# A two-layer decoder on one core: decayed scores kept in PSUM, one round a unit in layer 1 self-attention, and a copy pinned to its place

## The chip, the core and the metric

The kernel runs on one core of a Trainium2 chip. The core has a matrix engine (PE, TensorE), a vector engine (DVE, VectorE), an activation engine (ACT, ScalarE), a general engine (POOL, GpSimd) and an engine that here only issues transfers (SP, SyncE). Each works through its own instructions in order and waits on semaphores for the others. Data lie in device memory, in SBUF (128 partitions), or in PSUM, the memory into which PE writes and from which DVE and ACT read its products. The profile lists PE's weight loads as a line of their own, PEld, since they overlap the matmuls.

The metric is the time of one execution in device microseconds. The time before is the median of three runs. One further execution was recorded by the profiler; every duration here is from that one.

## What is computed

The input is 8 sequences of 512 tokens with 256 features, and for each a context of 64 rows. Two decoder layers follow, each with three sub-blocks, and after each sub-block a layernorm of the sum of its input and its output:

```python
x = layernorm(x + L0_attn(x, ...))    # 16 heads of 16, latent keys and values, decay
x = layernorm(x + L0_xattn(x, ctx, ctx, mask))
x = layernorm(x + L0_ffn(x, ...))     # butterfly products around a gelu
x = layernorm(x + L1_attn(x, ...))    # 16 heads of 64, causal, rotary, latent keys and values
x = layernorm(x + L1_xattn(x, ctx, ...))  # 8 heads of 64 over 512 + 64 keys
x = layernorm(x + L1_ffn(x, ...))     # 8 experts, the best 2 of each token
```

What matters here of the three sub-blocks that the change touches:

```python
# L0_attn: the decay multiplies the scores before the softmax
scores = einsum('bhqd,bhkd->bhqk', qh, k_rec) / sqrt(d)
decay = exp(-0.01 * abs(t[:, None] - t[None, :]))
attn = softmax(scores * decay)

# L1_attn: q and k are rotated, scores are causal
q = q * cos + rotate_half(q) * sin
scores = einsum('bhsd,bhtd->bhst', q, k) / sqrt(64) + causal
out = einsum('bhst,bhtd->bhsd', softmax(scores), v)

# L1_ffn: each token goes to two experts, weighted
w, idx = top_k(softmax(logits / 1.5), 2)
```

## The kernel before

The program is written in stages: layer 0 self-attention (about 22 to 800 us of the span), layer 0 context attention and feed-forward (to 1222), layer 1 self-attention (to 2105), layer 1 context attention with the routing of tokens to experts in it (to 2935), the experts (to 3464), and the last stores. In most stages PE's instructions run in the order in which the program writes them (`manual_schedule` for PE). On the other engines a scheduler places instructions by its own estimate of when their inputs are ready, and it can move one ahead of others; `keep_in_program_order` around an instruction holds it where it is written. Tiles come from pools: a tag has a number of buffers, and the next tile of the tag waits until the buffer's old content has had its last reader.

**Layer 0 self-attention.** A unit is a sequence b and a group g of four heads, 32 units. Each unit goes through `l0_project` (q and k, s_qk), `l0_maxima` for four query tiles i, `l0_shift`, then for four key tiles kt `l0_probs` and `l0_values`, and `l0_finish`. The units are interleaved: step kt of unit n does `l0_probs` of unit n, `l0_values` of the step before, and `l0_maxima` of unit n+2; then one piece of another unit, `l0_shift` (transposes tM, L463), `l0_finish` (transposes tO, L520), `l0_project` (s_qk, L415 and L416), or a part of an output projection (tT L539, o_out L547) or of the preparation of the next sequence (tT L378, o_lat L386).

`l0_maxima` (L423) computes scores for 128 queries against 512 keys, four heads as two pairs. Each pair has one PSUM tile s_sc of two banks. On DVE one `tensor_tensor_reduce` for each head (L437) multiplies by the decay table, writes the decayed scores to SBUF (`scored`) and the row's maximum to mx. After both pairs, one `tensor_tensor` (L447) takes the diagonal 128x128 blocks of all four heads less the maxima into diag. `l0_probs` (L472) later puts the transposed scores of two pairs into two PSUM tiles s_st: off the diagonal they are computed afresh with the decay factored into the rows (L481 and L484, with kf, kr, qf, qr, which POOL multiplies out in L468), on the diagonal diag is transposed in (L486). ACT exponentiates them to pt (L490), and `l0_values` multiplies (L501). s_sc, s_st and s_qk take turns in three two-bank PSUM buffers. POOL in this stage also multiplies out the butterfly factors for the feed-forward (L308), which it runs nearly without pause.

Ahead of the first unit, the product o_wlat of two weights is copied to `wlat` by DVE (L586), and o_lat (L386) needs it.

**Layer 1 self-attention.** A unit is a sequence b and a pair c of heads, 64 units. The four query tiles form groups m: tiles 0 and 1, tile 2, tile 3 (`GROUPS`). `l1_scores` (L939) makes s_sc (L949) and the softmax: DVE adds the mask and takes the maximum (L279), ACT exponentiates (L290), DVE scales (L926). `l1_transposes` transposes p on PE (tP, L981) and copies with ACT (L982). `l1_values` (L995) multiplies with v (o_pv, L1005), after the last group `out_done` copies to aT, and after the last pair of a sequence an output projection follows (o_out, L248) in two pieces that are put off, and with it residual and layernorm on DVE and POOL. `l1_prepare` makes q and k (s_q, L880 and L881), their rotation on DVE (L885, L886) and by four accumulating transfers from POOL's queue (L889), and v (t_v, L896). A unit is done in two steps: step 0 does group 0, step 1 groups 1 and 2. In each step PE does the scores, a piece of preparation (`l1_pre`: s_q of the unit two on, or t_v of the next one), the transposes of the step before, and the values of the step before that.

**Layer 1 context attention.** 128 steps of s_sc (L1130), a softmax, transposes (tP, copied to pt by DVE and ACT at L108 and L110) and o_pv (L1164, L1172), with projections of the next unit (t_qk L1084, k completed by POOL copies at L1092, t_v L1097). The routing of sequence b is done in pieces among the steps of sequence b+1. `route_norm` (L1216) writes the layernorm into z, which has one buffer. `route_picks` (L1271) writes the expert weights into z (L1282) and the token numbers (L1283, a copy of 4 columns from `tokens_at`, which is there from the start). `route_places` (L1286) finds rows and sends z out with eight indirect transfers from POOL's queue (rows_in, L1307). The experts' loads of rows_in (xr, L1430) follow all those they need.

Of the kernel before, what the change touches and what calls it, by code (L numbers as in the profile page):

```python
# [11 lines left out]
F32 = mybir.dt.float32  # L12
I32 = mybir.dt.int32
AF = mybir.ActivationFunctionType
ALU = mybir.AluOpType
# [3 lines left out]
P = 128  # L19
# [30 lines left out]
def decoder_kernel(ctx: ExitStack, tc: tile.TileContext, a: dict, out: bass.AP):  # L50
# [35 lines left out]
    def slot(name):  # L86
        return ring.tile([P, SLOT], F32, tag="slot", name=name)
# [335 lines left out]
    def l0_maxima(b, g, i):  # L423


        q, k = live["qk", b, g]
        mx = live["mx", b, g]
        for pair in range(2):
            s = s_tile("s_sc")
            for j in range(2):  # L430
                h = 32 * (2 * pair + j)
                pe.matmul(  # L432
                    s[:, j, :], lhsT=q[h : h + 32, i * P : (i + 1) * P], rhs=k[h : h + 32, :], start=True, stop=True
                )
            for j in range(2):
                h = 2 * pair + j
                dve.tensor_tensor_reduce(  # L437
                    out=scored[:, h, :],
                    in0=s[:, j, :],
                    in1=decay[:, i, :],  # L440
                    scale=1.0,
                    scalar=-3.0e38,
                    op0=ALU.mult,
                    op1=ALU.max,
                    accum_out=mx[:, i, h : h + 1],
                )
        dve.tensor_tensor(  # L447
            live["diag", b, g][:, i],
            scored[:, :, i * P : (i + 1) * P],
            mx[:, i, :].unsqueeze(2).to_broadcast([P, 4, P]),  # L450
            ALU.subtract,
        )

    def l0_shift(b, g):

# [100 lines left out]
    with tc.tile_pool(name="bfly", bufs=1, side="right") as bfly, phase("l0_self") as ph, psum("a", 3, 1, 1):  # L556

        vaug = [ph.tile([P, NT, 288], F32, name=f"vaug{n}", bufs=1) for n in range(2)]
        mneg = ph.tile([P, NT, P], F32, name="mneg", bufs=1)
        pool.memset(mneg, 0.0)  # L560
        for n in range(2):
            pool.memset(vaug[n], 1.0)

        scored = slot("scored").rearrange("p (h n) -> p h n", h=4)
        diags = [slot(f"diag{i}").rearrange("p (i h n) -> p i h n", i=NT, h=4) for i in range(2)]
        bias_row = bfly.tile([1, 1024], F32, name="bias_row")
        sp.dma_start(out=bias_row, in_=a["ff_bexp"].rearrange("(o n) -> o n", o=1))
        butterfly = butterfly_ops(bfly, bias_row)
        units = [(b, g) for b in range(NB) for g in range(4)]
        later, scalings = [], []  # L570
        with tc.manual_schedule(engines={PE}):
            turn0, turn1, latent, values = l0_prepare(0)
            turn0()
            turn1()
            dve.tensor_tensor(wkT, wkT, wvT, ALU.add)
            o = o_tile("o_wlat")
            for c in range(KC):
                for k in range(KC):
                    pe.matmul(
                        o[:, c * 64 : (c + 1) * 64],  # L580
                        lhsT=wkT[:, k, c * P : (c + 1) * P],
                        rhs=wdown[:, k, :],
                        start=(k == 0),
                        stop=(k == KC - 1),
                    )
            dve.tensor_copy(wlat.rearrange("p c n -> p (c n)"), o[:, 0 : KC * 64])  # L586
            latent()
            l0_project(*units[0])

            between = [values, partial(l0_project, *units[1])]  # L590
            for i in range(NT):
                l0_maxima(*units[0], i)
                if between:
                    between.pop(0)()
            l0_shift(*units[0])
            l0_project(*units[2])

            for i in range(2):
                l0_maxima(*units[1], i)
        for n, (b, g) in enumerate(units):  # L600

            maxima = [(*units[n + 2], i) for i in range(NT)] if n + 2 < len(units) else []
            if n == 0:
                maxima = [(*units[1], i) for i in range(2, NT)] + maxima
            if g == 0 and b + 1 < NB:
                later.extend(l0_prepare(b + 1))
            for kt in range(NT):
                l0_probs(b, g, kt)

                if kt:  # L610
                    l0_values(b, g, kt - 1)
                elif n:
                    l0_values(*units[n - 1], NT - 1)
                for _ in range(-(-len(maxima) // (NT - kt))):
                    l0_maxima(*maxima.pop(0))

                if kt == 1 and n + 1 < len(units):
                    l0_shift(*units[n + 1])
                if kt == 1:

                    if scalings:
                        scalings.pop(0)(tc.keep_in_program_order)
                elif kt == 2:
                    if n:
                        l0_finish(*units[n - 1])
                        if g == 0:
                            later.extend(l0_output(b - 1))
                else:
                    if kt and n + 3 < len(units):
                        l0_project(*units[n + 3])  # L630
                    if later:
                        later.pop(0)()
                for _ in range(3 - kt % 2):
                    next(butterfly, None)
        l0_values(*units[-1], NT - 1)
        l0_finish(*units[-1])
        later.extend(l0_output(NB - 1))
        for piece in later:
            piece()
        for scaling in scalings:  # L640
            scaling()
        for _ in butterfly:
            pass
        o = o_tile("o_bias")
        for f in range(8):
            pe.matmul(o[:, f : f + 1], lhsT=bias_row[0:1, f * P : (f + 1) * P], rhs=one, start=True, stop=True)
        dve.tensor_tensor(upb, o[:, 0:8], upb, ALU.add)
# [258 lines left out]

    GROUPS = ((0, 1), (2,), (3,))

    STEPS = ((0,), (1, 2))

    def l1_pre(b, c, step):

        at = units.index((b, c))
        if step == 0 and at + 2 < len(units):
            pieces_of[units[at + 2]].pop(-2)()
        if step == 1 and at + 1 < len(units):
            pieces_of[units[at + 1]].pop()()
        if c == 5 and b + 1 < NB:
            pieces_of[b + 1, 0].pop(0)()

    def scaled(p, sums, n):

        rsum = col("rsum", 4)
# [3 lines left out]

    put_off = []

    def groups(stage):  # L930


        def run(b, c, step):
            for m in STEPS[step]:
                stage(b, c, m)

        return run

    def l1_scores(b, c, m):  # L939
        q, k, _ = live["qkv", b, c]  # L940
        s = s_tile("s_sc")
        p = p_tile(bufs=4)
        sums = col("sums", 4)
        at = 0
        for i in GROUPS[m]:
# [46 lines left out]
            if then:  # L992
                then(b)

    def l1_values(b, c, m):  # L995
        pt = live.pop(("pt", b, c, m))
        _, _, v = live["qkv", b, c]
        if m == 0:
            live["o", b, c] = o_tile("o_pv")
        o = live["o", b, c]  # L1000
        n = 0
        for k, block in enumerate(l1_blocks(m)):
            cols = slice(block[0][0] * P, (block[-1][0] + 1) * P)
            for j in range(2):
                pe.matmul(  # L1005
                    o[64 * j : 64 * (j + 1), cols],
                    lhsT=v[:, k, 64 * j : 64 * (j + 1)],
                    rhs=pt[:, j, n : n + len(block), :].rearrange("p k n -> p (k n)"),
                    start=(k == 0),
                    stop=(k == GROUPS[m][-1]),  # L1010
                )
            n += len(block)
        if m == len(GROUPS) - 1:
            out_done(b, c, live.pop(("o", b, c)), woT1, 8, lambda: xs[b])

    with phase("l1_self") as ph, tc.manual_schedule(engines={PE}):
        for u, what in ((0, 0), (0, 0), (0, 0), (0, 0), (1, 0)):
            pieces_of[units[u]].pop(what)()
        _pipeline(
            [(b, c, step) for b in range(NB) for c in range(8) for step in range(len(STEPS))],  # L1020
            [
                (0, groups(l1_scores)),
                (0, l1_pre),
                (1, groups(l1_transposes)),
                (2, groups(l1_values)),
            ],
            put_off,
        )


    q1_k1 = slot("q1_k1")
# [239 lines left out]
    def route_picks(b):  # L1271
# [8 lines left out]
        both, z = picked[:, 0:NT, :], live["z", b]  # L1280
        dve.tensor_tensor(both, picks[0], picks[1], ALU.add)
        dve.tensor_tensor(z[:, :, D : D + NE], both, pr, ALU.mult)  # L1282
        dve.tensor_copy(z[:, :, D + NE], tokens_at[:, b * NT : (b + 1) * NT])  # L1283
        live["picks", b] = picks, picked

    def route_places(b):  # L1286
# [358 lines left out]
```

## Time and profile before

| | us |
|---|---|
| median of 3 runs | 3511.45 (3504.51 to 3514.59) |
| profiled execution | 3503.39 |
| its span | 3501.7 |
| layer 0 self-attention, stretch 100 to 750 | 650 |
| layer 1 self-attention, 1222 to 2105 | 883 |
| layer 1 context attention, 2105 to 2935 | 830 |
| PE busy in the span | 3299.3 (94%) |
| DVE / ACT / POOL busy | 2087.4 (60%) / 1510.5 (43%) / 1118.1 (32%) |
| mean granted PE clock | 0.973 of full speed |

In the lines that follow, a row of a list of instructions in time has its start and its duration in us, the engine, the source line, the operation, the tile written and the tiles read, shapes, how many instructions of one kind were put together (x4), and in brackets the idle time of the engine before it with what ended it. A row of the waits has the waiting engine and line, what it waited for, the sum in us, how often, and the longest. A share of busy time is an average over stages with different limits; what a stage gains or loses is read inside it.

### The profile page before, as it was taken

To read this page: it belongs to the slowest core of one execution; us is meant where nothing else is said; L and a number is where in the kernel's file an instruction comes from. 1 tells how busy PE (TensorE), PEld (TensorE's weight loads), DVE (VectorE), ACT (ScalarE), POOL (GpSimd) and SP (SyncE) were. 2 spreads that over 40 slices of the span, in tenths; PEclk is the share of its full clock that TensorE was granted. 3 is DMA by queue.
4 is the path that set the end of the run, shared out by engine and by line. 5 is a ranking of instruction groups with operands and counts; after the bars stand their busy time and mean duration, and the time that the engine had idled before them with its cause. 6 is when DMAs were issued, how large, how long until landed. Compare 5 with 4: busy or idle time off the path is not lost. (4 is left out here: it accounts for less than half of the span.)

```text
span 3501.7 us, 52528 instructions
## 1 busy us (share of the span) xinstructions
PE 3299.3 (94%) x19574; PEld 2080.0 (59%) x19574; DVE 2087.4 (60%) x5710; ACT 1510.5 (43%) x3139; POOL 1118.1 (32%) x1032
## 2 busy tenths in 40 slices
PE   7999999998999989999999999999999999999995
PEld 3344344445666656666666665555555556888884
DVE  5777777767666467677776775666666664111112
ACT  2444444453344255565555663444444343222222
POOL 3888788862211122222222210011111111222222
PEclk8999999998999999999999999999999999999997
DMA  4001011110000099232322320000000004666674
GB/s 134 25 25 33 21 35 42 40 63 13 2 2 1 13 252 243 37 43 37 42 39 37 43 43 4 10 13 22 19 19 19 10 19 167 193 188 181 188 229 138
DMA packets 166002, 234.96 MB, mean 67 GB/s; under 512 B 26570, under 2 KB 128650, under 8 KB 165747
## 3 DMA queue, kind: packets, MB, share of 16 engines
q1 hardware_dynamic: 139010, 175.83, 15.9%
q0 software_dynamic: 25584, 51.57, 10.3%
q10 hardware_dynamic: 1152, 4.19, 0.3%
q8 instruction: 156, 2.56, 0.3%
q14 instruction: 100, 0.81, 0.1%
HBM read 135.83 MB, written 61.11 MB: 56 GB/s over the span
## 5 line engine op out<-in xcount | busy, mean ns | idle before, releaser
L437 DVE CUSTOM_DVE_ANT_0 scored<-s_sc,decay 128x512 f32<-128x512 f32 x512 | 323.0, 687 | 179.6 <-PE s_sc L432 178.8
L290 ACT ACTIVATE p<-p,nm 128x128 f32<-128x128 f32 (+3 forms) x512 | 282.5, 553 | 301.9 <-DVE nm L279 300.4
L889 POOL DMA_DIRECT2D qk<-turned x256 | 208.2, 1231 | 591.8 <-issue 296.0
L490 ACT ACTIVATE pt<-s_st 128x1024 f32<-128x1024 f32 x256 | 261.9, 1024 | 278.4 <-PE s_st L486 250.3
L926 DVE TENSOR_SCALAR p<-p,rsum 128x576 f32<-128x576 f32 (+4 forms) x768 | 300.3, 433 | 10.0
L1135 ACT ACTIVATE p<-s_sc,nm 128x576 f32<-128x576 f32 x256 | 189.6, 743 | 222.3 <-DVE nm L1134 201.3
L1501 DVE TENSOR_SCALAR y<-o_y,share 128x256 f32<-128x256 f32 x71 | 34.3, 484 | 408.6 <-PE o_y L1481 408.6
L1464 PE MATMUL s_h<-xnT,we 128*128 128x256 f32 (+1 forms) x1248 | 260.3, 362 | 0.0
L279 DVE CUSTOM_DVE_ANT_0 p<-s_sc,tabs 128x128 f32<-128x128 f32 (+3 forms) x512 | 225.2, 484 | 56.7 <-PE s_sc L949 56.6
L1481 PE MATMUL o_y<-we,h 128*128 128x256 f32 x1136 | 251.4, 379 | 0.0
L1502 POOL DMA_INDIRECT total<-y,to x71 | 110.2, 1553 | 388.4 <-DVE y L1501 220.4
L1481 PEld LDWEIGHTS o_y<-we,h 128*128 128x128 f32 x1136 | 215.3, 190 | 29.0
L1464 PEld LDWEIGHTS s_h<-xnT,we 128*128 128x128 f32 x1248 | 216.7, 191 | 24.3 <-ACT xnT L1443 0.2
L1134 DVE TENSOR_REDUCE nm<-s_sc 128x1 f32<-128x576 f32 x256 | 183.3, 749 | 73.0 <-PE s_sc L1130 72.1
L110 ACT COPY pt<-tP 128x512 f32<-128x512 f32 (+1 forms) x224 | 109.9, 491 | 208.3 <-PE tP L1147 118.5
L982 ACT COPY pt<-tP 128x384 f32<-128x384 f32 (+1 forms) x384 | 172.9, 513 | 43.6 <-PE tP L981 43.1
L949 PE MATMUL s_sc<-qk 64*128 64x128 f32 (+3 forms) x1024 | 176.4, 459 | 14.3 <-DMA qk<-turned 10.3
L1130 PE MATMUL s_sc<-k,q 64*128 64x288 f32 x1024 | 170.0, 442 | 7.7 <-ACT p L1135 7.5
L981 PE MATMUL tP<-ident,p 128*128 128x128 f32 x1280 | 169.4, 276 | 5.9 <-ACT pt L982 4.5
L981 PEld LDWEIGHTS tP<-ident,p 128*128 128x128 f32 x1280 | 144.5, 141 | 49.9 <-issue 27.7
L447 DVE TENSOR_TENSOR diag<-scored,mx 128x512 f32<-128x512 f32 x128 | 167.5, 1309 | 2.4
L1005 PE MATMUL o_pv<-pt,vc 128*64 128x128 f32 (+1 forms) x2304 | 167.5, 290 | 0.0
(280 smaller groups left out, 6445.9 us busy)
## 6 DMA issues: line engine op xcount, KB each, us to landing
we<-in_mo_w SPq DMA_DIRECT2D x78, 1024.0 KB
rows_in<-zero SPq DMA_DIRECT2D x64, 530.0 KB
qk<-turned POOLq DMA_DIRECT2D x256, 128.0 KB, 4.5
coef<-in_ff_upw SPq DMA_DIRECT2D x40, 256.0 KB
coef<-in_ff_dnw SPq DMA_DIRECT2D x40, 256.0 KB
xr<-rows_in SPq DMA_DIRECT2D x32, 265.0 KB
x<-in_x SPq DMA_DIRECT2D x8, 512.0 KB
total<-x SPq DMA_DIRECT2D x8, 512.0 KB
```

The costliest lines, as they stand in the source:

```text
L279: dve.tensor_tensor_reduce(out=p[:, j, 0:n], in0=s[:, j, 0:n], in1=m, scale=-scale, scalar=3.0e38, op0=ALU.add, op1=ALU.min, accum_out=nm[ ...
L290: act.activation(p[:, j, 0:n], p[:, j, 0:n], AF.Exp, bias=nm[:, j : j + 1], scale=-1.0, accum_out=sums[:, at + j : at + j + 1],)
L437: dve.tensor_tensor_reduce(out=scored[:, h, :], in0=s[:, j, :], in1=decay[:, i, :], scale=1.0, scalar=-3.0e38, op0=ALU.mult, op1=ALU.max, ...
L490: tc.keep_in_program_order(act.activation(pt, s, AF.Exp, scale=1.0 / 16.0))
L889: pool.dma_start(out=qk[h : h + 32], in_=other[g : g + 32], accum_op=ALU.add)
L926: dve.tensor_scalar(p[:, j, 0:n], p[:, j, 0:n], rsum[:, j : j + 1], None, ALU.mult)
L949: pe.matmul(s[:, j, at : at + n], lhsT=q[h : h + 64, i * P : (i + 1) * P], rhs=k[h : h + 64, 0:n], start=True, stop=True,)
L981: pe.transpose(t[:, n, :], p[:, j, at * P : (at + 1) * P], ident)
L1134: dve.tensor_reduce(nm[:, j : j + 1], s, AX.XY, ALU.max, negate=True)
L1135: act.activation(p[:, j, :].rearrange("p (t n) -> p t n", t=2), s, AF.Exp, bias=nm[:, j : j + 1], accum_out=sums[:, j : j + 1])
L1464: pe.matmul(s[:, j, :], lhsT=w1[:, c, f * P : (f + 1) * P], rhs=xnT[:, c, :], start=(c == 0), stop=(c == KC - 1),)
L1481: pe.matmul(o, lhsT=h[:, f, i * P : (i + 1) * P], rhs=w2[:, f, :], start=(f == 0), stop=(f == 7),)
```

## The change

There are four edits.

- In `l0_maxima` the reduction writes the decayed scores back into the PSUM tile s that it reads. The diagonal less the maxima is taken from there, in two instructions, one for each pair, inside the loop over pairs. The SBUF tile `scored` is gone.
- The copy of o_wlat into `wlat` moves from DVE to ACT.
- In layer 1 self-attention `_pipeline` with two steps a unit becomes a loop over units with one round each. A round computes scores of groups 1 and 2 of this unit, a shared preparation piece where there is one, t_v of the next unit, s_q of the unit two on, all transposes of the unit before (groups 1, 2, 0), a put-off piece of an output projection where there is one, the scores of group 0 of this unit, and all values of the unit before in one run. p has a tag for each group, with the width of that group.
- The copy of the token numbers into z is held in program order, directly behind the product that is written into z.

```diff
@@ -435,7 +435,7 @@
             for j in range(2):
                 h = 2 * pair + j
                 dve.tensor_tensor_reduce(
-                    out=scored[:, h, :],
+                    out=s[:, j, :],
                     in0=s[:, j, :],
                     in1=decay[:, i, :],
                     scale=1.0,
@@ -444,12 +444,12 @@
                     op1=ALU.max,
                     accum_out=mx[:, i, h : h + 1],
                 )
-        dve.tensor_tensor(
-            live["diag", b, g][:, i],
-            scored[:, :, i * P : (i + 1) * P],
-            mx[:, i, :].unsqueeze(2).to_broadcast([P, 4, P]),
-            ALU.subtract,
-        )
+            dve.tensor_tensor(
+                live["diag", b, g][:, i, 2 * pair : 2 * pair + 2],
+                s[:, :, i * P : (i + 1) * P],
+                mx[:, i, 2 * pair : 2 * pair + 2].unsqueeze(2).to_broadcast([P, 2, P]),
+                ALU.subtract,
+            )
 
     def l0_shift(b, g):
 
@@ -561,7 +561,6 @@
         for n in range(2):
             pool.memset(vaug[n], 1.0)
 
-        scored = slot("scored").rearrange("p (h n) -> p h n", h=4)
         diags = [slot(f"diag{i}").rearrange("p (i h n) -> p i h n", i=NT, h=4) for i in range(2)]
         bias_row = bfly.tile([1, 1024], F32, name="bias_row")
         sp.dma_start(out=bias_row, in_=a["ff_bexp"].rearrange("(o n) -> o n", o=1))
@@ -583,7 +582,7 @@
                         start=(k == 0),
                         stop=(k == KC - 1),
                     )
-            dve.tensor_copy(wlat.rearrange("p c n -> p (c n)"), o[:, 0 : KC * 64])
+            act.copy(wlat.rearrange("p c n -> p (c n)"), o[:, 0 : KC * 64])
             latent()
             l0_project(*units[0])
 
@@ -906,18 +905,6 @@
 
     GROUPS = ((0, 1), (2,), (3,))
 
-    STEPS = ((0,), (1, 2))
-
-    def l1_pre(b, c, step):
-
-        at = units.index((b, c))
-        if step == 0 and at + 2 < len(units):
-            pieces_of[units[at + 2]].pop(-2)()
-        if step == 1 and at + 1 < len(units):
-            pieces_of[units[at + 1]].pop()()
-        if c == 5 and b + 1 < NB:
-            pieces_of[b + 1, 0].pop(0)()
-
     def scaled(p, sums, n):
 
         rsum = col("rsum", 4)
@@ -927,19 +914,11 @@
 
     put_off = []
 
-    def groups(stage):
-
-
-        def run(b, c, step):
-            for m in STEPS[step]:
-                stage(b, c, m)
-
-        return run
-
     def l1_scores(b, c, m):
         q, k, _ = live["qkv", b, c]
         s = s_tile("s_sc")
-        p = p_tile(bufs=4)
+        width = sum(i + 1 for i in GROUPS[m]) * P
+        p = ph.tile([P, 2, width], F32, tag=f"p{m}", name="p")
         sums = col("sums", 4)
         at = 0
         for i in GROUPS[m]:
@@ -992,40 +971,58 @@
             if then:
                 then(b)
 
-    def l1_values(b, c, m):
-        pt = live.pop(("pt", b, c, m))
-        _, _, v = live["qkv", b, c]
-        if m == 0:
-            live["o", b, c] = o_tile("o_pv")
-        o = live["o", b, c]
-        n = 0
-        for k, block in enumerate(l1_blocks(m)):
-            cols = slice(block[0][0] * P, (block[-1][0] + 1) * P)
-            for j in range(2):
-                pe.matmul(
-                    o[64 * j : 64 * (j + 1), cols],
-                    lhsT=v[:, k, 64 * j : 64 * (j + 1)],
-                    rhs=pt[:, j, n : n + len(block), :].rearrange("p k n -> p (k n)"),
-                    start=(k == 0),
-                    stop=(k == GROUPS[m][-1]),
-                )
-            n += len(block)
-        if m == len(GROUPS) - 1:
-            out_done(b, c, live.pop(("o", b, c)), woT1, 8, lambda: xs[b])
+    def l1_values(b, c):
+        _, _, v = live.pop(("qkv", b, c))
+        o = o_tile("o_pv")
+        for m in BEHIND:
+            pt = live.pop(("pt", b, c, m))
+            n = 0
+            for k, block in enumerate(l1_blocks(m)):
+                cols = slice(block[0][0] * P, (block[-1][0] + 1) * P)
+                for j in range(2):
+                    pe.matmul(
+                        o[64 * j : 64 * (j + 1), cols],
+                        lhsT=v[:, k, 64 * j : 64 * (j + 1)],
+                        rhs=pt[:, j, n : n + len(block), :].rearrange("p k n -> p (k n)"),
+                        start=(k == 0),
+                        stop=(k == GROUPS[m][-1]),
+                    )
+                n += len(block)
+        out_done(b, c, o, woT1, 8, lambda: xs[b])
+
+
+    BEHIND = (1, 2, 0)
 
     with phase("l1_self") as ph, tc.manual_schedule(engines={PE}):
         for u, what in ((0, 0), (0, 0), (0, 0), (0, 0), (1, 0)):
             pieces_of[units[u]].pop(what)()
-        _pipeline(
-            [(b, c, step) for b in range(NB) for c in range(8) for step in range(len(STEPS))],
-            [
-                (0, groups(l1_scores)),
-                (0, l1_pre),
-                (1, groups(l1_transposes)),
-                (2, groups(l1_values)),
-            ],
-            put_off,
-        )
+        for at in range(len(units) + 1):
+            this = units[at] if at < len(units) else None
+            before = units[at - 1] if at else None
+            if this:
+                b, c = this
+                shared = pieces_of[b + 1, 0] if c == 5 and b + 1 < NB else []
+                l1_scores(*this, 1)
+                l1_scores(*this, 2)
+                if shared:
+                    shared.pop(0)()
+                if at + 1 < len(units):
+                    pieces_of[units[at + 1]].pop()()
+                if at + 2 < len(units):
+                    pieces_of[units[at + 2]].pop(-2)()
+            if before:
+                for m in BEHIND:
+                    l1_transposes(*before, m)
+            if this:
+                if shared:
+                    shared.pop(0)()
+                if put_off:
+                    put_off.pop(0)()
+                l1_scores(*this, 0)
+            if before:
+                l1_values(*before)
+        while put_off:
+            put_off.pop(0)()
 
 
     q1_k1 = slot("q1_k1")
@@ -1280,7 +1277,8 @@
         both, z = picked[:, 0:NT, :], live["z", b]
         dve.tensor_tensor(both, picks[0], picks[1], ALU.add)
         dve.tensor_tensor(z[:, :, D : D + NE], both, pr, ALU.mult)
-        dve.tensor_copy(z[:, :, D + NE], tokens_at[:, b * NT : (b + 1) * NT])
+
+        tc.keep_in_program_order(dve.tensor_copy(z[:, :, D + NE], tokens_at[:, b * NT : (b + 1) * NT]))
         live["picks", b] = picks, picked
 
     def route_places(b):
```

## The prediction

> **What bounds the kernel now.** I read the engine totals first (PE busy 94% of the span), then busy time by stage, then in each stage the waits, the timeline of one period, and the order of instructions. A stage is moved only by what moves its PE.
>
> ```profile
> 100.00:750.00 650.00, 625.23 (x4212) 265.21 (x4212) 486.66 (x1179) 309.86 (x369) 530.82 (x396) 0.99 0.11 33
> ...
> 1222.00:2105.00 883.00, 850.22 (x6065) 575.63 (x6066) 634.53 (x2078) 514.89 (x1516) 221.11 (x266) 0.99 0.45 82
> 2105.00:2935.00 830.00, 777.24 (x4184) 448.68 (x4182) 542.78 (x1336) 343.27 (x816) 103.20 (x148) 0.97 0.06 18
> ```
>
> Each line is a stretch, its length, busy PE, PEld, DVE, ACT, POOL, and the granted clock: layer 0 self-attention, layer 1 self-attention, layer 1 context attention. PE leads everywhere, but a busy figure hides short waits of matmuls that overlap. One step of layer 0 shows them:
>
> ```profile
> 442.69 0.49 PE L481 MATMUL s_st<-qr,kf 32*128 32x128 f32 x4
> 444.21 0.38 PE L481 MATMUL s_st<-qr,kf 32*128 32x128 f32 x2 [1.03 <-DVE mx L437]
> ...
> 442.86 0.68 DVE L437 CUSTOM_DVE_ANT_0 scored<-s_sc,decay 128x512 f32<-128x512 f32 x1
> 443.47 0.08 DVE L437 DVE_READ_ACCUMULATOR2_ANT mx<- 128x1 f32 x1
> 443.47 0.68 DVE L437 CUSTOM_DVE_ANT_0 scored<-s_sc,decay 128x512 f32<-128x512 f32 x1
> 444.08 0.08 DVE L437 DVE_READ_ACCUMULATOR2_ANT mx<- 128x1 f32 x1
> ...
> 444.69 0.68 DVE L437 CUSTOM_DVE_ANT_0 scored<-s_sc,decay 128x512 f32<-128x512 f32 x1
> 445.30 0.08 DVE L437 DVE_READ_ACCUMULATOR2_ANT mx<- 128x1 f32 x1
> 445.41 0.69 DVE L447 TENSOR_TENSOR diag<-scored,mx 128x512 f32<-128x512 f32 x1
> ```
>
> The second half of s_st (heads 2 and 3) starts 0.13 us after the second score reduction's accumulator read: it takes over the PSUM buffer of the first s_sc pair. Reductions with no wait between them start 0.61 apart; diag, which waits for the last maximum, starts 0.72 after it. What PE waited there in the stretch (44 times, longest 3.9; matmuls that overlap hide more), and the worst diag:
>
> ```profile
> PE s_st L481 <- DVE mx L437: 21.5, 44, 3.9
> ```
>
> ```profile
> 406.16 9.39 DVE L447 TENSOR_TENSOR diag<-scored,mx 128x512 f32<-128x512 f32 x1
> ...
> 417.06 0.58 PE L481 MATMUL s_st<-qr,kf 32*128 32x128 f32 x2 [3.91 <-DVE mx L437]
> ```
>
> In layer 1 context attention DVE itself stands, seven times, 44.1 us in all, and PE behind it:
>
> ```profile
> 2307.32 0.96 POOL L1307 DMA_INDIRECT rows_in<-z,irow  x1 [1.93 <-DMA rows_in<-z,irow]
> ...
> 2309.98 0.17 DVE L1283 COPY z<-tokens_at 128x4 f32<-128x4 f32 x1 [6.13 <-DMA rows_in<-z,irow]
> ...
> 2312.58 3.78 PE L1084 MATMUL t_qk<-xT,q_k 128*128 128x512 f32 x4 [3.94 <-DVE pt L108]
> ```
>
> Four matmuls of t_qk that take 1.98 us elsewhere take 3.78 here: after the gap the clock is granted at 0.5. Layer 1 self-attention has one wait of the kind, in the units with an out projection:
>
> ```profile
> PE s_q L880 <- DVE nm L279: 12.2, 7, 2.9
> ```
>
> **Part 1, layer 0's scores.** Now the s_sc buffer is released by the last maximum of its pair. After the change the diag of that pair still reads it, so it is released behind one more instruction. I walked the timeline from the start of s_sc in an undisturbed step: reductions start at 1.18, 1.79, 2.40, 3.01, second half of s_st at 2.54, next s_sc at 4.97. After the change reductions of one pair write one tile, so the second waits for the first, and diag waits for the second. A waited start is 0.73 after the one before (the 0.72 to 0.73 of diag above), so: 1.18, 1.91, diag at 2.64. A half diag is 128x256 with a PSUM input; the nearest row is att (L524), 411 ns. It ends at 3.05; 0.06 for PE to see it gives 3.11 against 2.54, that is +0.57 us. It binds where the matmuls in front of it on PE (the transposes tM, tO or tT of one neighbour) are done by 2.5: 29+29+13 = 71 of the 128 steps. 71 x 0.565 = 40. Steps with four or more matmuls of another unit in front arrive at 2.95 to 3.01 (13 steps, 1.7 in all); those behind one more transpose group, and those with nothing in front, add some 3. The six maxima groups of the prelude, each half a microsecond later, add 3. **+48**. The second pair's buffer is released at about 5.39 with q's addition in front of the last reduction, against 5.54 for the next s_sc: hidden, with 0.15 to spare.
>
> The reduction that writes PSUM has no row: every DVE instruction of the trace writes SBUF. Bounds: reading PSUM costs nothing extra (q with a PSUM input 683 ns, diag without one 682 at its shortest), so I take 0, by symmetry. The other end is a second pass over the elements: 683 less 411 is 272 ns per 256 columns, so 0.54 per reduction, two of them on the chain, 71 times: +77. A gain has only the wait to come from: if the waited starts cost nothing, 0.12 less a step, -8.5.
>
> [...]
>
> What the change gives in layer 0: diag has two SBUF inputs now, and its duration runs from 682 to 9393 ns with a mean of 1366, while POOL works on two SBUF inputs beside it (the 9.39 us lies over L308's pairs). After, one input is in PSUM. But PE does not wait on diag: in the step walk, the time above the undisturbed step is 15.7 us in the whole stage, of which three places belong to a long diag, 6.4 (at 410, with the 3.91 gap above), 1.3 and 1.0, and the rest mostly to the layernorm's round trip to POOL, which stays. With the clock behind the large gap: **-10** (0 to -15.7). POOL may run faster; PE waits on it for 2 us in all.
>
> **Part 2, the prelude's wlat copy.** o_lat waits 4.63 us at 14.08 for that copy, which stands on DVE behind decay-table scalings that wait for DMA. ACT is free at 8.5 and the product ends at 9.45. The tables and weights may bind next: **-2** (0 to -4.1).
>
> **Part 3, one round a unit in layer 1.** Instructions are the same, their order on PE is not. Group intervals of a unit (11.165 us, 64 units) that the order touches: s_sc to o_pv work in two pieces, 1.679 + 0.801 = 2.480, against 2.329 for the one place where 18 o_pv matmuls stand together: -0.15. The 20 transposes in one run take 1.703 + 0.748 = 2.451 now in two; three t buffers and ACT copies of 476 and 589 ns give about 2.5: +0.05. Net -0.1, -6.5 us in all (0 to -16). At the units with an out projection DVE does residual and layernorm, and PE's s_q (12.2 us in 7 waits now, line above) would wait about 2.2 each, 3 more, some of it with the clock. The waits of tP and s_sc (4.9 and 4.0) can go. **-5** (-16 to +8). DVE has about 10.1 us of work in a unit of 11.2, so it covers the new order only narrowly.
>
> **Part 4, the pinned copy.** The copy of batch b+1 was placed right behind the scatters of batch b; z has one buffer, so DVE, in order, stands until the last scatter landed: 5.7 to 7.2 us, seven times. Queued behind it are pt, rsum and nm, and PE waits for these: 3.94, 3.82, 2.92, 1.51, 3.93, 4.01 and 5.78, 25.9 in sum, and behind each the clock is at 0.5 for 3.4 to 6.8 us, some 16 us lost. A second way: the two steps that hold it take 16.1, 16.0, 15.9, 13.4, 16.0 and 15.3 us against 9.55 in the batch without one, 35.4 more, and 7.6 at the end: 43. After, the copy stands behind the product into z of its own batch, 0.17 us without a wait, and the first writer of z is the layernorm's scaling, some 50 us behind the scatters. Nothing is late next: POOL's k copies that also queue behind scatters are for a k two rounds on, and the first expert's rows, asked for at 2927.67, land by 2936 while PE would come at 2934.4, with the clock's help before that. **-43** (-26, the gaps alone, to -60, the whole 44.1 and the clock).
>
> **Sum.** +48 -10 -2 -5 -43 = -12. The profiled execution took 3503.39 (span 3501.7 and 1.7 around it), 8.1 under the median 3511.45 of three. 3503.4 - 12 = 3491.4, and against the median 3511.45 - 12 = 3499.5: I say 3500.
>
> **Rivals.**
> A. The reduction into PSUM is slower. For: no row shows such a write. Against: reading PSUM is free. Each 0.1 us is 142 x 0.1 = 14 us; from 0.16 a reduction (22 us) the whole is more than 0.3% slower; at a second pass +77, 3577. Ends on the other side.
> B. The release is hidden: waited starts cost nothing and PE makes up the rest, because steps not bound absorb the shift. Against: the undisturbed step repeats to 0.01 us, so PE has no slack there. Then only the gains stay: -60, 3451.
> C. Layer 1 self-attention turns DVE-bound: the narrow cover of part 3 is gone and PE waits 0.5 us a unit. 64 x 0.5 = 32 instead of -5: net +25, 3536. For: 10.1 of 11.2. Against: the order of DVE's work within a unit leaves reductions directly behind their scores.
> D. The pin frees nothing because POOL's scatters still pace DVE's next routing piece: then +48 -17 = +31, 3542. Against: 50 us of distance.
>
> **How the numbers follow.** The sum as walked 0.46 (3500; -12 lies next to the bound of 0.3%, 10.5 us, about what this kernel's runs can tell from no change, so 0.25 faster, 0.18 same, 0.03 slower); A 0.28 (0.24 slower, 0.04 same); B 0.14 (faster); C 0.09 and D 0.03 (0.05 same, 0.06 slower, 0.01 faster). Faster 0.40, same 0.27, slower 0.33. The range 3465 to 3548 leaves out the outer half of B and of A.
>
> **What would show it.** Right: in layer 0 the undisturbed step at 5.54 instead of 4.97, second half of s_st 0.06 behind the half diag, half diags near 0.41 and never above 1; reductions at 687 still. In context attention no DVE wait on rows_in and no half clock there. In layer 1 a unit of 11.07. Wrong: a reduction above 0.75; a clock under 0.97 in layer 0, whose PE gap per step grows to about 1 us (gaps of 1.03 left the clock alone so far, 3.91 did not); waits of s_q or tP on DVE in most units.

## The result and the profile after

The changed kernel took 3538.19 us (median of four runs, 3536.83 to 3540.47); beside it the kernel before took 3507.98 (four runs, 3502.37 to 3514.59). The ratio is 1.0086 with a 95% interval of 1.0065 to 1.0107: slower by about 30 us, where I had forecast 12 less. The time lies inside my range, the sign is wrong; that it lies inside is luck, since the parts below miss in both directions.

The span grew from 3501.7 to 3535.1 us. Cut at the first and last matmuls of named lines, it falls apart like this:

| stretch | before | after | change | forecast |
|---|---|---|---|---|
| ahead of the first s_sc | 21.8 | 18.3 | -3.5 | -2 |
| layer 0 self-attention, to its last o_out | 779.2 | 861.5 | +82.3 | +38 |
| layer 0 context attention and feed-forward | 437.7 | 443.9 | +6.2 | 0 |
| layer 1 self-attention, to its last o_pv | 860.6 | 846.9 | -13.7 | -5 |
| layer 1 context attention, first t_qk to last o_pv | 811.4 | 776.1 | -35.3 | -43 |
| experts, first transpose to last o_y | 520.2 | 517.4 | -2.8 | 0 |

As stretches of busy time, first layer 0 self-attention before, then four of the cuts after (columns: length, then busy PE, PEld, DVE, ACT, POOL, granted clock, and two of DMA):

```profile
21.80:802.00 780.20, 741.64 (x4906) 317.64 (x4906) 558.29 (x1371) 356.07 (x424) 589.52 (x441) 0.97 0.13 39
```

```profile
18.30:881.00 862.70, 772.58 (x4906) 332.23 (x4906) 542.30 (x1499) 355.85 (x424) 542.43 (x441) 0.95 0.13 37
881.00:1323.70 442.70, 413.14 (x1830) 286.68 (x1829) 269.88 (x492) 156.32 (x191) 80.13 (x83) 0.94 0.05 13
1323.70:2194.00 870.30, 848.39 (x6108) 585.14 (x6109) 632.88 (x2082) 517.23 (x1517) 211.01 (x262) 0.99 0.43 78
2194.00:2970.00 776.00, 748.02 (x4114) 434.32 (x4112) 536.77 (x1318) 341.63 (x813) 101.95 (x143) 0.98 0.05 17
```

The 4906 matmul records of layer 0 self-attention are as many as before. DVE's busy time in the stretch fell from 558 to 542 us and POOL's from 590 to 542, and still it is 82 us longer. PE was busy 742 us there before and 773 after: the added time is 51 us of idle PE and 31 us of matmuls that ran at a lower clock or overlapped less.

An undisturbed step is one in which nothing but the step's own work holds PE up. One of them before, on PE:

```profile
369.17 1.16 PE L432 MATMUL s_sc<-k,q 32*128 32x512 f32 x8
...
371.72 0.48 PE L481 MATMUL s_st<-qr,kf 32*128 32x256 f32 x2 [0.17 <-DVE mx L437]
...
374.15 1.16 PE L432 MATMUL s_sc<-k,q 32*128 32x512 f32 x8
```

One after, on PE and on DVE, from s_sc at 442.38 to the next at 448.05:

```profile
442.38 1.16 PE L432 MATMUL s_sc<-k,q 32*128 32x512 f32 x8
443.47 0.66 PE L520 MATMUL tO<-ident,oT 128*128 128x128 f32 x4
444.06 0.92 PE L481 MATMUL s_st<-qr,kf 32*128 32x384 f32 x4
445.62 0.91 PE L481 MATMUL s_st<-qr,kf 32*128 32x384 f32 x4 [0.65 <-DVE diag L447]
...
448.05 1.16 PE L432 MATMUL s_sc<-k,q 32*128 32x512 f32 x8
```

```profile
443.56 0.70 DVE L437 CUSTOM_DVE_ANT_0 s_sc<-s_sc,decay 128x512 f32<-128x512 f32 x1 [1.33 <-PE s_sc L432]
444.17 0.14 DVE L437 DVE_READ_ACCUMULATOR2_ANT mx<- 128x1 f32 x1
444.35 0.70 DVE L437 CUSTOM_DVE_ANT_0 s_sc<-s_sc,decay 128x512 f32<-128x512 f32 x1
444.97 0.14 DVE L437 DVE_READ_ACCUMULATOR2_ANT mx<- 128x1 f32 x1
445.14 0.42 DVE L447 TENSOR_TENSOR diag<-s_sc,mx 128x256 f32<-128x256 f32 x1
```

The step is 5.67 us long; it was 4.97 to 4.98. PE's second half of s_st starts 0.06 behind the half diag, as forecast, but at 3.24 from the start of s_sc and not at 3.11. A reduction that waits for the one before it starts 0.79 behind it, and its accumulator read takes 0.14 where it took 0.08.

The waits in the stretch 100 to 800 us after, of layer 0 self-attention (the 44 waits before are of 100 to 750):

```profile
PEld s_st L481 <- DVE diag L447: 93.4, 69, 2.3
...
PE s_st L481 <- DVE diag L447: 63.1, 69, 2.1
PEld s_sc L432 <- DVE diag L447: 62.0, 74, 0.8
```

The 44 waits of PE on a maximum, 21.5 us, have become 69 waits on a diag, 63.1 us. In five steps, where a layernorm's round trip to POOL delays the first reduction, the wait is longer; one of them:

```profile
479.75 0.66 PE L486 MATMUL s_st<-ident,diag 128*128 128x128 f32 x4
480.34 1.06 PE L501 MATMUL o_pv<-pt,vaug 128*32 128x512 f32 x8
...
485.23 0.38 PE L481 MATMUL s_st<-qr,kf 32*128 32x128 f32 x2 [1.73 <-DVE diag L447]
...
486.36 1.12 PE L486 MATMUL s_st<-ident,diag 128*128 128x128 f32 x4
487.41 1.91 PE L501 MATMUL o_pv<-pt,vaug 128*32 128x512 f32 x8
```

Four diag transposes take 0.66 us and eight o_pv 1.06 in the step ahead (the first two lines); behind the wait they take 1.12 and 1.91. The granted clock says why, before (a step of the same kind, whose wait was 1.03) and after:

```profile
446.00:449.00 3.00, 3.00 (x24) 1.04 (x16) 1.28 (x4) 2.81 (x5) 2.46 (x2) 1.00 0.00 1
```

```profile
486.00:489.00 3.00, 3.00 (x16) 0.92 (x12) 1.05 (x3) 1.02 (x1) 2.35 (x2) 0.50 0.00 1
```

The pinned copy, after, and PE's waits in layer 1 context attention:

```profile
L1281 DVE COPY z<-tokens_at x8: 163/165/166, 2354.4 to 3010.6; 128x4 f32<-128x4 f32 x8
its engine sat idle before it (us, times) until:
who waited for it (us, times):
```

```profile
PE tZ L1227 <- DVE pt L108: 17.0, 7, 2.8
PE t_v L1094 <- DVE pt L108: 4.7, 8, 0.8
PE s_sc L1127 <- ACT p L1132: 3.1, 4, 1.5
```

Nothing stands between the two headings of the first answer: nobody waits, in either direction. The four waits of t_qk (15.7 us) and the long one of o_pv (5.8) are gone; those of tZ on pt, 17.0 us, were there before with the same sum.

Layer 1 self-attention, one unit after:

```profile
1732.99 1.77 PE L928 MATMUL s_sc<-qk 64*128 64x384 f32 x8
1734.69 1.16 PE L895 MATMUL t_v<-vu,lat 128*128 128x128 f32 x8
1735.69 1.88 PE L879 MATMUL s_q<-xT,wqT 128*128 128x512 f32 x4
1737.41 1.02 PE L880 MATMUL s_q<-lat,kd_ku 128*128 128x512 f32 x2
1738.26 2.54 PE L960 MATMUL tP<-ident,p 128*128 128x128 f32 x20
1740.73 0.93 PE L928 MATMUL s_sc<-qk 64*128 64x128 f32 x8
1741.59 2.40 PE L983 MATMUL o_pv<-pt,vc 128*64 128x128 f32 x36
1743.91 1.77 PE L928 MATMUL s_sc<-qk 64*128 64x384 f32 x8
```

From s_sc to s_sc it is 10.92 us, against 11.165. No wait stands inside it.

### The profile page after: what moved, and what is told of

Same layout as the page of the kernel before. It is cut to its first block, busy times and chain, and to the rows that moved or that the text cites. A ratio compares the mean times of both kernels' runs of the same rounds, so it can differ in the third digit from the quotient of the medians.

```text
span 3535.1 us, 52615 instructions
## 1 busy us (share of the span) xinstructions
PE 3315.9 (94%) x19574; PEld 2099.1 (59%) x19574; DVE 2071.4 (59%) x5837; ACT 1512.9 (43%) x3140; POOL 1067.0 (30%) x1032
## 5 line engine op out<-in xcount | busy, mean ns | idle before, releaser
L437 DVE CUSTOM_DVE_ANT_0 s_sc<-s_sc,decay 128x512 f32<-128x512 f32 x512 | 356.3, 697 | 270.3 <-PE s_sc L432 263.5
L290 ACT ACTIVATE p<-p,nm 128x384 f32<-128x384 f32 (+3 forms) x512 | 282.4, 552 | 256.5 <-DVE nm L279 256.5
L279 DVE CUSTOM_DVE_ANT_0 p<-s_sc,tabs 128x384 f32<-128x384 f32 (+3 forms) x512 | 225.1, 484 | 45.1 <-PE s_sc L928 43.1
L1462 PEld LDWEIGHTS s_h<-xnT,we 128*128 128x128 f32 x1248 | 215.4, 190 | 23.9 <-ACT xnT L1441 0.2
L481 PE MATMUL s_st<-qr,kf 32*128 32x128 f32 (+2 forms) x768 | 131.1, 431 | 72.2 <-DVE diag L447 71.7
L928 PE MATMUL s_sc<-qk 64*128 64x384 f32 (+3 forms) x1024 | 178.6, 460 | 14.9 <-DMA qk<-turned 9.7
L432 PE MATMUL s_sc<-k,q 32*128 32x512 f32 x1024 | 160.0, 665 | 7.6 <-DVE diag L447 4.6
```

The source lines that it names most:

```text
L279: dve.tensor_tensor_reduce(out=p[:, j, 0:n], in0=s[:, j, 0:n], in1=m, scale=-scale, scalar=3.0e38, op0=ALU.add, op1=ALU.min, accum_out=nm[ ...
L290: act.activation(p[:, j, 0:n], p[:, j, 0:n], AF.Exp, bias=nm[:, j : j + 1], scale=-1.0, accum_out=sums[:, at + j : at + j + 1],)
L437: dve.tensor_tensor_reduce(out=s[:, j, :], in0=s[:, j, :], in1=decay[:, i, :], scale=1.0, scalar=-3.0e38, op0=ALU.mult, op1=ALU.max, accum ...
L1462: pe.matmul(s[:, j, :], lhsT=w1[:, c, f * P : (f + 1) * P], rhs=xnT[:, c, :], start=(c == 0), stop=(c == KC - 1),)
```

## The experiments

Four kernels take the change apart, each beside the kernel before on the same chip (four runs of each; seven of the kernel before, median 3502.3, 3500.71 to 3507.83).

**The pin alone.**

```diff
-        dve.tensor_copy(z[:, :, D + NE], tokens_at[:, b * NT : (b + 1) * NT])
+        tc.keep_in_program_order(dve.tensor_copy(z[:, :, D + NE], tokens_at[:, b * NT : (b + 1) * NT]))
```

> The kernel before with only the token-number copy held in its place. Theory (the pin is worth what the context attention stage lost between the two profiles, 811.5 to 776.1 us): 35 us less than before, about 3473; no DVE wait on rows_in, no matmul of t_qk behind a gap of 3.8 us, everything ahead of the stage as before. Rival (the stage only lost because the other edits shifted it): within 10 us of before. By my forecast's own term it would be 43 less.

Measured: 3469.07 us (3463.69 to 3470.76), ratio 0.9903 (0.9887 to 0.992), 33 less. The edit carries its gain alone. In its profiled execution, the fastest of its four, the stage took 767.6 us, 43.8 less than before. With the same instructions it took 776.1 in the changed kernel, and PE's larger waits have the same sums there (tZ 17.0 in both, t_v 4.6 and 4.7, s_sc 3.1 in both); what differs is the time lost to the clock in that stage (length of each stretch below full clock times what it was below, counted whole in the stage in which it begins): 5.1 us here, 15.4 there, 27.3 before. In the third kernel with the edit, all but the scores, the stage took 770.2 and lost 8.5. So the stage gave 35, 41 and 44 us in three profiles, against my 43; the 33 is what the median of the whole kernel's time fell by.

**The scores alone.**

```diff
-                    out=scored[:, h, :],
+                    out=s[:, j, :],
...
-        dve.tensor_tensor(
-            live["diag", b, g][:, i],
-            scored[:, :, i * P : (i + 1) * P],
-            mx[:, i, :].unsqueeze(2).to_broadcast([P, 4, P]),
-            ALU.subtract,
-        )
+            dve.tensor_tensor(
+                live["diag", b, g][:, i, 2 * pair : 2 * pair + 2],
+                s[:, :, i * P : (i + 1) * P],
+                mx[:, i, 2 * pair : 2 * pair + 2].unsqueeze(2).to_broadcast([P, 2, P]),
+                ALU.subtract,
+            )
...
```

> The kernel before with only layer 0's scores written back into PSUM and the diagonals taken from there. Theory (this edit alone carries the loss; layer 0 self-attention grew from 779 to 862 us between the profiles, and the stage behind it by 6): 80 to 90 us more than before, about 3595; the undisturbed step 5.67 us instead of 4.97. Rival (the edits disturb each other, and each alone is small): under 50 more, the forecast's 38 among them.

Measured: 3584.75 (3580.71 to 3589.85), ratio 1.0229 (1.0212 to 1.0247), 82 more. The undisturbed step is 5.67. This edit alone is the whole loss. Layer 0 self-attention took 858.5 us, and the stage behind it 443.2.

**The round alone.** The diff is the layer 1 part of the change as shown above.

> The kernel before with only the one-round order of layer 1 self-attention. Theory: a unit of 10.92 us instead of 11.165, less what the units with an out projection wait more: 14 us less, about 3494. Rival (my forecast's term): 5 less. A rival C in which DVE becomes the bound would be 20 or more slower.

Measured: 3488.91 (3485.35 to 3492.39), ratio 0.9955 (0.9938 to 0.9972), 13 less.

**All but the scores.** The changed kernel with `scored` and the one diag behind both pairs put back; the diff is that of the scores alone, reversed.

> The changed kernel with layer 0's scores as before (in SBUF, one diag behind both pairs); pin, round and the copy on ACT stay. If the parts add: -35 for the pin, -14 for the round, -3 for the copy, about -52, 3456, and faster than both kernels. If the parts only help beside the slower layer 0, less than 30.

Measured: 3451.41 (3444.54 to 3460.55), ratio 0.986 (0.9842 to 0.9878), 51 less than before and faster than both kernels. The parts add: 82.4 - 13.4 - 33.2 - 4 for the copy on ACT = +32, against +30 measured for the whole change. The copy was not run alone; its 4 us is read from the profiles: the time ahead of the first s_sc is 18.3 and 17.7 us in the two kernels that have it and 21.5 to 23.3 in the seven others, the kernel before among them.

Three more kernels ask what it is in the scores edit. They ran twice each, beside two runs of the kernel before (3508.64 and 3510.99).

**Half diags from SBUF.**

```diff
-        dve.tensor_tensor(
-            live["diag", b, g][:, i],
-            scored[:, :, i * P : (i + 1) * P],
-            mx[:, i, :].unsqueeze(2).to_broadcast([P, 4, P]),
+            dve.tensor_tensor(
+                live["diag", b, g][:, i, 2 * pair : 2 * pair + 2],
+                scored[:, 2 * pair : 2 * pair + 2, i * P : (i + 1) * P],
+                mx[:, i, 2 * pair : 2 * pair + 2].unsqueeze(2).to_broadcast([P, 2, P]),
...
```

> The kernel before with diag taken for each pair, from the scores in SBUF; reductions write SBUF. The PSUM tile is released by the second reduction, as before. Theory (what costs is that the tile is held until its diag has read it): undisturbed step 4.97 us and second half of s_st at 2.54, as before; total within 15 us of before, and half diags long where POOL works beside them. Rival (cutting diag in two and waiting twice is the cost): step 5.3 or more.

Measured: 3559.29, ratio 1.0141 (1.0097 to 1.0185), 49 more. The 29 steps with tM in front have a median of 4.98, as in the kernel before, so cutting diag in two costs nothing by itself; but the 29 with tO in front, 4.97 before, have 5.27, and the total was wrong. The diags say why: in every one of those 29 steps the first half diag takes 1.46 us or more. This kernel:

```profile
L447 DVE TENSOR_TENSOR diag<-scored,mx x256: 415/1057/9598, 25.3 to 815.9; 128x256 f32<-128x256 f32 x128
```

and after:

```profile
L447 DVE TENSOR_TENSOR diag<-s_sc,mx x256: 412/424/426, 24.4 to 839.7; 128x256 f32<-128x256 f32 x128
```

Shortest, median and longest duration in ns: with both inputs in SBUF, half the work of before is as long as 9.6 us, from PSUM it is never above 0.43. In this kernel the long diag of the first pair stands in front of the second pair's reductions, so the next s_sc waits for them; in the kernel before it comes last in the step and PE has the time. In the kernel before, the nine diags with none of POOL's instructions beside them take 691 to 694 ns, the 119 others 682 to 9393 with a median of 1358; the longest spans seven of POOL's instructions that began after it, and ends 0.55 us behind the last. After, the half diags from PSUM take 412 to 426 ns beside POOL's work (163 of them) and 414 to 426 without (93). So the long diags fall together with POOL's work, and those from PSUM are as short beside it. What couples the two is not shown: no run here takes POOL's work away.

**The undecayed diagonal from PSUM.** Reductions write SBUF as before, each half diag reads s.

```diff
...
+            dve.tensor_tensor(
+                live["diag", b, g][:, i, 2 * pair : 2 * pair + 2],
+                s[:, :, i * P : (i + 1) * P],
+                mx[:, i, 2 * pair : 2 * pair + 2].unsqueeze(2).to_broadcast([P, 2, P]),
...
```

> The kernel before, reductions write SBUF, but diag of each pair reads the undecayed scores from PSUM: the decay is left out on the diagonal blocks. The tile is held as in the changed kernel, and nothing but PE writes PSUM. Theory: reductions 0.61 apart with no wait, diag 0.73 behind the second, 0.42 long, seen 0.06 later: second half of s_st at 1.79+0.73+0.42+0.06 = 3.00 against 2.54 before and 3.24 after; step 5.43, and about 71 x 0.46 = 33 us and some more than before. Rival (writing PSUM is the whole cost): step 4.97.

Measured: 3547.55, ratio 1.0107 (1.0064 to 1.0151), 38 more. PE in one step:

```profile
344.13 1.16 PE L432 MATMUL s_sc<-k,q 32*128 32x512 f32 x8
...
347.13 0.48 PE L481 MATMUL s_st<-qr,kf 32*128 32x256 f32 x2 [0.63 <-DVE diag L447]
...
349.57 1.16 PE L432 MATMUL s_sc<-k,q 32*128 32x512 f32 x8
```

The second half of s_st comes 3.00 behind s_sc and the step is 5.44: both as written down. Nothing writes PSUM here but PE, so two thirds of the longer step (0.46 of 0.70) are the holding of the tile, with the wait of diag behind the second reduction in it.

**Writing PSUM without reading it.** Reductions write back into s, one diag behind both pairs reads the decay table in SBUF.

```diff
-                    out=scored[:, h, :],
+                    out=s[:, j, :],
...
-            scored[:, :, i * P : (i + 1) * P],
+            decay[:, :, i * P : (i + 1) * P],
...
```

> The kernel before, reductions write back into PSUM as in the changed kernel, but one diag behind both pairs, and it reads the decay table in SBUF in place of the scores: the scores are left out on the diagonal blocks. No tile is held for a diag. Theory: the second reduction of a pair waits for the first (0.79 behind it, as in the changed kernel), and its accumulator read takes 0.14 instead of 0.08, which releases the tile: second half of s_st at 1.97+0.61+0.14+0.06 = 2.78, step 5.21, about 71 x 0.24 = 17 us more than before. [...] Rival (writing PSUM disturbs PE): step 5.6 and longer matmuls.

Measured: 3552.33, ratio 1.0121 (1.0078 to 1.0165), 42 more. The step:

```profile
331.66 1.16 PE L432 MATMUL s_sc<-k,q 32*128 32x512 f32 x8
...
334.44 0.91 PE L481 MATMUL s_st<-qr,kf 32*128 32x384 f32 x4 [0.19 <-DVE mx L437]
...
336.86 1.16 PE L432 MATMUL s_sc<-k,q 32*128 32x512 f32 x8
```

2.78 and 5.20: as written down, 0.24 of the 0.70, and no matmul is longer. With the kernel ahead, 0.46 + 0.24 = 0.70 accounts for the step of the changed kernel. The total is far above the 17 us of the undisturbed steps: layer 0 self-attention grew by 42.3 us, and 39.3 us there are lost to the clock where it was 22.2 before (counted as above), while its diag still has two SBUF inputs and takes up to 8 us. How the other part of this surplus divides I did not settle.

## Why the prediction was wrong, point by point

**Part 1 failed: the cost of layer 0's scores was put at +48, with -10 of gains; it was +82.** The mechanism was the one forecast, and the two kernels above show it to a hundredth of a microsecond in the undisturbed step: the tile is held until its diag has read it and the second reduction waits for the first, and this binds where few matmuls stand in front. The sum was mis-sized in four terms, of which the first, the price of writing PSUM, was put at nothing though no row showed it.

- The step. I put the waited start behind a reduction at 0.73, from a reduction that writes SBUF. Behind one that writes PSUM it is 0.79, twice in the chain: 0.70 a step and not 0.565, 10 us over 71 steps. Reading PSUM costs nothing extra (683 ns against 682), and from that I took writing for free "by symmetry". That was the wrong choice. The reductions themselves hardly changed (median 686 to 699 ns), so rival A, a slower reduction, is not what happened. The 0.06 lies in the accumulator read behind the reduction: its median is 83 ns before and in the kernel that only reads PSUM a second time, 141 after and in the kernel that only writes PSUM, and a waited start comes 0.03 us behind its end before and after. Why that read ends later is not shown. The wait on a reduction has its own price in these rows: behind one that writes SBUF the next start comes 0.61 us later without a wait on it, and 0.73 with one.
- The steps I had called barely bound. Those with s_qk and a transpose group in front put the second half of s_st into the buffer of the second pair, not the first, which comes free later still: 14 steps grew by 0.35, not 0.1. Those with tT in front grew by 0.81, with o_lat by 0.38, with o_out by 0.32. All undisturbed steps together give 58 x 0.70 + 7 x 0.81 + 6 x 0.73 + 7 x 0.38 + 14 x 0.35 + 6 x 0.32 + 4.3 for the rest = 64.5, where I had 45.
- The prelude, up to the first full step: 12.9 more, where I had 3.
- The clock. In the five steps behind a layernorm the wait of PE on L481 grew from about 1.05 to about 1.74 us, and in four of them half clock (granted at 0.5) follows it (one in the lines above); these five and one more tT step with half clock behind its wait grew by 7.6 beyond the 6 x 0.73 above. I had named this as a thing that would make the forecast wrong, and put no price on it. The stage behind, unchanged, lost 32.4 us to the clock where it had lost 23.9, which covers its +6.2; in the four other kernels with a longer layer 0 it lost 25.6 to 30.7 and grew by 2.2 to 5.5.

The gain from diag's input in PSUM was about right: the three places with a long diag, 8.7 of the 10 us, are gone. 64.5 + 12.9 + 7.6 - 8.7 = 76; the other 6 are in the last steps and in further stretches of half clock, not told apart.

**Part 2** said -2 (0 to -4.1); -3.5 was measured. **Part 3** said -5 (-16 to +8); -13.7, and 13 less when run alone. The merged o_pv gave the 0.15 I had, the 20 transposes cost 0.01 and not 0.05 (2.465 against 2.451), and one gain was not seen: s_q's first four matmuls, now behind t_v and not behind s_sc, take 1.719 and not 1.821 us. The units with an out projection wait as long as before, 11.7 us in 7 waits of s_q, and 3.5 more at s_sc; the 2.2 each that I had allowed for did not come. Rival C did not happen.

**Part 4** said -43 (-26 to -60); -35.3 in the profile, 33 less alone, 43.8 in one execution. The mechanism was right, and nothing took the wait's place; rival D did not happen. The clock's share, put at 16, came out at 12 in the changed kernel and at 22 and 19 in the two others with the edit (27.3 less what each lost). What varies is the half clock behind the tZ waits, whose sum is the same before and after: three stretches of it before, five in the changed kernel, two and three in the others.

**The sum.** Rival B, hidden release, is out. The forecast said 12 us faster because one term of four was about half of what it came to (38 against 82). The other three together came 2 us from their sum (52.5 against 50), and that is luck: part 3 gave 8.7 more than its term and part 4 7.7 less.

## What to carry to other kernels

Before an instruction is moved so that it reads a buffer a second time, ask who waits for that buffer: here PE's start moved by 0.70 us (0.42 of reading, the rest two waits) in 58 steps, and with the other steps and the clock this cost 82 us in a stage in which DVE and POOL had less work than before. A price that no row shows is not nothing because its mirror image is: bound it and look for the start-to-start gap, not the duration. When the parts of a change are independent, run them apart: three of these four together take 51 us off, and without the fourth the kernel takes 3451 us.

## What the runs showed of the hardware

- A DVE reduction that writes PSUM takes nearly as long as one that writes SBUF (medians 699 and 686 ns), but what waits for it starts 0.79 us behind its start and not 0.73; its accumulator read takes 141 ns and not 83.
- The clock and the length of PE's gap. Between 100 and 2900 us of the span of the changed kernel, of the gaps that began at full clock, none of 65 from 0.6 to 1.0 us was followed by half clock within 2 us of its end, 2 of 15 from 1.0 to 1.3, 3 of 5 from 1.3 to 1.6, 9 of 16 from 1.6 to 2.0, 7 of 8 from 2 to 3, and both above 3. So between 1 and 3 us it went either way, and one stage with the same instructions lost 5.1, 8.5 and 15.4 us to it in three kernels. The stretches at half clock between 100 and 2900 us last 3.41 us or a multiple of it (6.83, 13.65 and 17.07).
